# A graph layer on one core: the map to the output moves into the free columns of a PSUM bank that the next range's sums use

## The chip, the cores and the metric

The kernel runs on one core of a Trainium2 chip. Its time is the device time of one execution in microseconds (us). Three timed runs of the kernel before stand at 3958.60, 3969.82 and 3968.54 us, median 3968.54. All durations come from one profiled execution.

## The reference

12,500 nodes of 160 numbers, 400,000 edges sorted by target. Each node row is normalised, cut at zero and mapped; each edge takes its source's mapped row, multiplies it by weights that a small net makes of the edge's 16 features, and by its 4 attributes; the results are summed by target node, mapped to 160 outputs, and added to the node with a skip map:

```
h = maximum(layernorm(x), 0)
y = maps of h;  w = silu(e16 @ W1) @ W2          # per node; per edge
mid = products of w, y[src] and the 4 attributes  # per edge
z = zeros.at[dst].add(mid) / sqrt(10)             # per target node
out = x + C_S * (skip map of h) + C_X * (z @ W_l2)
```

## The kernel before, in words

A first stage (about 107 us) normalises and maps all nodes and writes the mapped rows to a table in memory, `y_d`. All that follows is one loop over 782 batches of four edge tiles (128 edges each, 3125 tiles). The order of every engine's instructions is that in which the code is written; engines wait for each other by semaphores alone.

What a batch b issues, in order: `weigh(b+2)` (edge weights on TensorE into a `pw` buffer, L606, and their scaling on ScalarE, L524); `products(b+1)` (VectorE: L620, L622, L529, L533; they need the gathered rows); the acts left `waiting` by an earlier batch; every 24 batches tables of offsets (`lowest`, `relate`, L199 to L238; the last time `any_far` with L242 and L243, too); `sums(b)`; the gathers (L571); `extras(b)`.

*Gathers.* POOL fetches the 128 source rows of a tile by one indirect transfer, `yg<-y_d,src_q`. A batch's first and third tile have a dependency written by hand (`gather`): the first waits for the last sums of the batch four earlier, the third for the second tile's sums of the batch three earlier. So rows keep step with the sums.

*Sums.* Edges are sorted, so a few tiles in a row touch few nodes. Such a range of 24, 12, 8, 6, 4 or 3 tiles (`wts_of`, from wide to narrow along the edges; 3 in the last 53 of 150 groups) is summed by one matmul per tile (L636) into columns 0 to 319 of a PSUM bank, `pz`. Two such banks alternate. When a range is through, VectorE turns the sums out of the bank with two transposes (L642, L643) into `za`, which holds the four ranges of a group.

*Groups.* A group is four ranges; with ranges of three tiles it is three batches. Before, in the first batch of the next group (k = 0), `linear` maps the group to 160 output columns: five matmuls (L649) into a `px` buffer, a copy to `os` on ScalarE (L651) and a placing matrix `place` on VectorE (L653). At k = 1 `add` places the rows by two matmuls (L661) into another `px` buffer, and `accumulate`, one batch later, adds them to the node's row in `acc` (L672, two instructions). `px` has two buffers, which the hidden layer (L585), the skip map and the look-ups also use. Early stores of finished nodes begin after batch `first_of[GE] + K - 1`.

Of the kernel before, what the change touches and what calls it, by code (L numbers as in the profile page):

```python
# [10 lines left out]
F32 = mybir.dt.float32  # L11
# [7 lines left out]
P = 128  # L19
M0 = 64  # L20
M1 = 32
D = M0 + 3 * M1
# [3 lines left out]
PC = 320  # L26
ZC = 448
ZK = 5
GT = 4
BT = 32  # L30
WN = 32
# [3 lines left out]
BLK = 96  # L35
# [16 lines left out]
def kernel(  # L52
# [34 lines left out]
    NG = len(glist)  # L87
    gstart.append(NG)
    NB = (T + GT - 1) // GT
# [29 lines left out]
    GE = NG - LATE  # L119
# [187 lines left out]
    def node_dma(g, n, dma):  # L307

        f = min(g + n, N // P) - g
        if f:  # L310
            dma(slice(g * P, (g + f) * P), slice(0, f), P)
        if f < n:
            dma(slice((g + f) * P, N), slice(f, f + 1), N - (g + f) * P)

    def store(g, n, eng):
        node_dma(g, n, lambda rows, t, p: eng.dma_start(by_tile(out[rows, :]), acc[:p, g + t.start:g + t.stop, :]))

    def by_tile(ap):
        n = ap.shape[0]
        return ap.rearrange("(t p) c -> p t c", p=min(P, n))  # L320
# [215 lines left out]
    with (  # L536
# [9 lines left out]
    ):  # L546
        hids, rows, wts, sels, z_ps, zT, o_sb, prs, sums_ps, summed = ({} for _ in range(10))
        xss, hss, sTs, sps, ohs, ohTs, vals, xTs = ({} for _ in range(8))
        halves = {}
# [12 lines left out]
        def windows_of(g):  # L562
            return -(-glist[g][2] // wts_of[glist[g][0]])
# [62 lines left out]
        def sums(b):  # L626
            pr, sel, g = prs.pop(b), sels.pop(b), group_of[b]
            q, lo, _ = glist[g]
            WT = wts_of[q]
            for k, t in enumerate(tiles_of(b)):  # L630
                w, o = divmod(t - lo, WT)
                if o == 0:
                    z_ps[g, w] = p_z.tile([P, 512], F32, name="pz")
                pz = z_ps[g, w]
                last = o == WT - 1 or t == T - 1
                mm = nc.tensor.matmul(pz[:, 0:PC], sel[:, slot(t), :, :], pr[:, slot(t), :], start=o == 0, stop=last)  # L636
                (halves if k == 1 else summed)[b] = mm.ins.name
                if last:
                    if w == 0:
                        zT[g] = post.tile([P, ZK, P], F32, name="za")  # L640
                    pz, at_w = z_ps.pop((g, w)), slice(WN * w, WN * (w + 1))
                    nc.vector.transpose(zT[g][:, :, at_w], pz[:, D:PC].rearrange("p (k u) -> p k u", k=ZK))  # L642
                    nc.vector.transpose(zT[g][0:32, :, at_w], pz[0:32, 0:D].rearrange("p (k u) -> p k u", k=ZK))  # L643

        def linear(g):
            m, za = WN * windows_of(g), zT.pop(g)
            po = p_x.tile([P, D], F32, name="px")
            for k in range(ZK):
                nc.tensor.matmul(po[:m, :], za[:, k, :m], wo[:, k, :], start=k == 0, stop=k == ZK - 1)  # L649
            os = post.tile([P, D], F32, name="os")  # L650
            nc.scalar.activation(os[:m, :], po[:m, :], AF.Copy)  # L651
            place = post.tile([P, 2, P], F32, name="place")
            nc.vector.tensor_scalar(place.rearrange("p h n -> p (h n)"), iota, at[:, g:g + 1], None, ALU.is_equal)  # L653
            o_sb[g] = os, place

        def add(g):
            m = WN * windows_of(g)
            os, place = o_sb.pop(g)
            ps = p_x.tile([P, 2, D], F32, name="px")
            for h in range(2):  # L660
                nc.tensor.matmul(ps[:, h, :], place[:m, h, :], os[:m, :], start=True, stop=True)  # L661
            sums_ps[g] = ps

        def accumulate(g):
            ps = sums_ps.pop(g)
            least = LOW if g >= GE else 0
            i = nc.values_load(tile_i[0:1, g:g + 1], engines=[mybir.EngineType.DVE], min_val=least, max_val=NT - 2,
                               skip_runtime_bounds_check_because="clamped to these bounds on the chip")
            part = acc[:, least:, :]
            for h in range(2):  # L670
                to = part[:, ds(i + h - least, 1), :]
                nc.vector.scalar_tensor_tensor(to, ps[:, h:h + 1, :], a_sb[:, ds(i + h, 1)], to,  # L672
                                               op0=ALU.mult, op1=ALU.add)
# [108 lines left out]
        SS, MAP = SB * XB + 8, 7  # L782
        xs_of = {x_batch(u) for u in range(XB)}

        K, KB = 3, BLK // GT
        waiting = []

        def left(act):

            if len(waiting) == 2:  # L790
                waiting.pop(0)()
            waiting.append(act)

        def extras(b):

            g = group_of[b]
            k = b - first_of[g]
            q, r = divmod(b, KB)
            u, v = divmod(b, SB)
            su, sv = divmod(b - SS, SK)  # L800
            if b % 2 == 0 and b + 4 < NB:
                s = (b + 4) // 2
                activate(s, hidden(s))
            if g and k == 0:
                linear(g - 1)
            if b == SS - 8:
                skip_load(0)
            skip = skips.get(sv) if 0 <= su < NU else None
            if skip and sv != MAP:
                skip(su)  # L810
            if r == KB - 11 and q + 1 < NQ:
                spread(q + 1, p_x.tile([P, MW], F32, name="px")[:, :windows_in(q + 1)])
            if u < XB:
                if v == 2:
                    hot_turn(u)
                elif v == 7:
                    x_center(u)
                elif v in (9, 10):
                    x_turn(u, HN * (v == 10))
                elif v == 11:  # L820
                    x_map(u, 0)
            if v == 1 and 0 < u <= XB:
                x_map(u - 1, HN)
            if g and k == 1:
                left(lambda: accumulate(g - 1))
                add(g - 1)
            if skip and sv == MAP:
                left(lambda: skip_add(su))
                skip(su)
# [21 lines left out]
        for b in range(NB):  # L851
            g = group_of[b]
            k = b - first_of[g]
            if b + EARLY < NB:
                features(b + EARLY)
            q, r = divmod(b, KB)
            if r == 0:
                e4_load(q + 1)
            if r == KB - 4:
                e4_join(q + 1)  # L860
            u, v = divmod(b, SB)
            su, sv = divmod(b - SS, SK)
# [16 lines left out]
            if early and b > first_of[GE] + K - 1:  # L879
                store(*early.pop(0), nc.sync)  # L880
# [12 lines left out]
        order.close()  # L893


# [2 lines left out]
    with (  # L898
# [5 lines left out]
        with tc.For_i(0, n, 1) as _:  # L904
# [8 lines left out]
            with tc.For_i(0, TP // GT, 1) as g:  # L913
# [32 lines left out]
                for k in range(GT):  # L946
# [4 lines left out]
                    m = fp.tile([P, ZC], F32, name="f_m")  # L951
# [29 lines left out]
            with tc.For_i(0, NT, 1) as i:  # L981
# [13 lines left out]
                po = fpp.tile([P, D], F32, name="f_po")  # L995
# [54 lines left out]
```

## Time and profile before

| what | value |
|---|---|
| median of three timed runs | 3968.54 us |
| profiled execution, its own time | 3957.18 us |
| its span, first to last instruction | 3955.3 us |
| granted TensorE clock, mean | 0.969 |
| first gather of the loop, last gather | 94.7 us, 3936.0 us |

A row of a group reads: line, engine, operation, output<-input, shape, count | busy us, mean ns of one | idle time just before them, and what ended most of it. A row of the waits reads: who <- whom: us in total, times, longest. A row of the timeline: start us, duration us, engine, line, operation, and in brackets the idle time before it and its releaser. A row of a stretch: from:to, its length, busy us of each engine with the count, granted TensorE clock, DMA share, GB/s; asked for one line of the kernel, it has the busy time of that line's engine alone. PE is TensorE, PEld its weight loads, DVE VectorE, ACT ScalarE, POOL GpSimd. A matmul of this kernel counts as two instructions there.

### The profile page before, as it was taken

The page shows a single profiled execution, that of the slowest core. Times are in us where ns is not written, and L with a number is a line of the kernel's source. Part 1 is how long each engine was busy: PE and PEld are TensorE (multiplying, and loading weights), DVE is VectorE, ACT ScalarE, POOL GpSimd, SP SyncE. Part 2 cuts the span into 40 slices and gives each one's busy share as a digit, 9 for nine tenths or more (in the row PEclk, how much of TensorE's full clock was granted, in tenths as well). Part 3 has the DMA queues.
Part 4 walks back from the last instruction along what each step waited for, and adds up shares of the span by engine and source line. Part 5 has one row for each costly group of instructions (what it writes and reads, how often), then busy time and mean ns, then how long its engine had stood idle before and what let it go on. Part 6 is the DMA issues. An engine that isn't in the chain of part 4 may idle for free.

```text
span 3955.3 us, 54096 instructions
## 1 busy us (share of the span) xinstructions
PE 3583.4 (91%) x17202; PEld 2316.8 (59%) x17202; DVE 2747.0 (69%) x6877; ACT 615.2 (16%) x1845; POOL 2963.8 (75%) x3144
## 2 busy tenths in 40 slices
PE   7898899999999888898989989998999989999988
PEld 7555555555566555555555655555655556666655
DVE  7566666666667666666667777777777777777776
ACT  6111111111111111111111111111111111111111
POOL 6777777777777777777777777777777777777766
PEclk9999999999999999999999999999999999999989
DMA  8222222222222322222222232222223222223224
GB/s 233 72 77 78 74 78 76 76 77 73 77 77 76 81 79 78 78 81 79 81 78 79 76 83 78 81 78 74 81 79 83 77 80 77 81 79 83 75 81 124
DMA packets 262503, 329.05 MB, mean 83 GB/s; under 512 B 82888, under 2 KB 212216, under 8 KB 262216
## 3 DMA queue, kind: packets, MB, share of 16 engines
q0 software_dynamic: 150128, 256.23, 24.2%
q1 hardware_dynamic: 111590, 69.02, 6.2%
q8 instruction: 141, 2.31, 0.2%
q14 instruction: 146, 1.20, 0.1%
q10 hardware_dynamic: 498, 0.30, 0.0%
HBM read 307.67 MB, written 17.61 MB: 82 GB/s over the span
## 4 chain that ended last, share of the span: by engine, by line
PE 38%; DMA 23%; DVE 20%; issue 12%; POOL 7%; DVEq 1%; SPq 1%; ACT 0%; POOLq 0%; ACTq 0%
DMA yg<-y_d,src_q 22%; PE pz L636 20%; DVE pr L533 7%; PE pw L606 7%; POOL yg L571 7%; DVE pr L529 5%; PE px L585 4%; PE px L649 3%; DVE acc L672 1%; DVE za L642 1%; DVE za L643 1%; PE px L661 1%; DVE at L215 1%; DMA acc<-in_x 1%; DVEq L672 0%
## 5 line engine op out<-in xcount | busy, mean ns | idle before, releaser
L571 POOL DMA_INDIRECT yg<-y_d,src_q x3061 | 2897.9, 947 | 950.5 <-issue 636.7
L636 PE MATMUL pz<-pr,sel 128*128 128x320 f32 x6250 | 1972.0, 460 | 23.7 <-DVE za L643 23.7
L636 PEld LDWEIGHTS pz<-pr,sel 128*128 128x128 f32 x6250 | 1165.0, 196 | 606.7 <-issue 239.3
L529 DVE TENSOR_TENSOR pr<-pw,yg 128x512 f32<-128x512 f32 x766 | 527.8, 689 | 919.9 <-DMA yg<-y_d,src_q 919.1
L606 PE MATMUL pw<-w,hT 64*128 64x192 f32 x6250 | 733.8, 353 | 253.3 <-DVE pr L533 222.6
L606 PEld LDWEIGHTS pw<-w,hT 64*128 64x128 f32 x6250 | 505.5, 189 | 548.0 <-issue 372.2
L533 DVE TENSOR_TENSOR pr<-pw,yg 128x384 f32<-128x384 f32 x1532 | 774.0, 546 | 0.0
L622 DVE TENSOR_TENSOR sel<-own,pw 128x512 f32<-128x512 f32 x782 | 536.7, 686 | 27.0
L585 PE MATMUL px<-xe,w 32*128 32x512 f32 x782 | 439.1, 642 | 24.8 <-issue 21.4
L590 ACT ACTIVATE hT<-px 128x512 f32<-128x512 f32 x391 | 233.3, 597 | 1308.7 <-PE px L585 1308.7
L524 ACT ACTIVATE pw<-ev 128x20 f32<-128x20 f32 x782 | 149.1, 191 | 1381.6 <-PE pw L606 1219.2
L642 DVE STREAM_TRANSPOSE za<-pz 128x160 f32<-128x160 f32 x598 | 202.5, 339 | 169.4 <-PE pz L636 167.8
L649 PEld LDWEIGHTS px<-wo,za 128*128 128x128 f32 x1500 | 213.8, 192 | 118.7 <-issue 66.6
L649 PE MATMUL px<-wo,za 128*128 128x160 f32 x1500 | 245.1, 311 | 19.0 <-DVE high L182 8.1
L585 PEld LDWEIGHTS px<-xe,w 32*128 32x128 f32 x782 | 114.5, 183 | 200.7 <-issue 187.8
L643 DVE STREAM_TRANSPOSE za<-pz 32x160 f32<-32x160 f32 x598 | 202.1, 338 | 20.5
L620 DVE TENSOR_TENSOR own<-iota,pw 128x128 f32<-128x128 f32 x782 | 198.3, 254 | 13.7 <-ACT pw L524 10.1
L672 DVE SCALAR_TENSOR_TENSOR acc<-px,a_sb,acc 128x160 f32 x300 | 113.6, 379 | 9.5 <-PE px L661 3.9
L661 PE MATMUL px<-os,place 128*128 128x160 f32 x600 | 113.1, 311 | 7.7 <-DVE place L653 4.8
L661 PEld LDWEIGHTS px<-os,place 128*128 128x128 f32 x600 | 91.6, 192 | 42.2 <-issue 25.4
L651 ACT ACTIVATE os<-px 128x160 f32<-128x160 f32 x150 | 45.5, 303 | 253.1 <-PE px L649 253.1
L347 POOL DMA_INDIRECT xr<-in_x,xi x64 | 61.0, 953 | 21.9 <-issue 11.9
(128 smaller groups left out, 1312.7 us busy)
## 6 DMA issues: line engine op xcount, KB each, us to landing
yg<-y_d,src_q POOLq DMA_INDIRECT x3061
xe<-in_e SPq DMA_DIRECT2D x784, 32.0 KB
xs<-in_x SPq DMA_DIRECT2D x48, 160.0 KB
acc<-in_x SPq DMA_DIRECT2D x11, 640.0 KB
y_d<-ys SPq DMA_DIRECT2D x11, 640.0 KB
out<-acc SPq DMA_DIRECT2D x11, 640.0 KB
raw<-in_e SPq DMA_DIRECT2D x32, 192.0 KB
src_q<-in_src SPq DMA_DIRECT2D x32, 48.0 KB
```

What stands on the lines that cost most here:

```text
L529: nc.vector.tensor_mul(pr[:, :n, :].rearrange("p t (x u) -> p t x u", x=2)[:, :, :, 0:M0], wt[:, :n, 0:NW].rearrange("p t (x u) -> p t x u ...
L533: nc.vector.tensor_mul(pr[:, :n, D * x + M0:D * (x + 1)].rearrange("p t (c u) -> p t c u", c=3), wt[:, :n, 96 * x + M0:96 * (x + 1)].unsqu ...
L571: fetch = nc.gpsimd.indirect_dma_start(out=yg[:, slot(t), :], out_offset=None, in_=y_d, in_offset=bass.IndirectOffsetOnAxis(ap=ev4[t // BL ...
L585: nc.tensor.matmul(ph, w1[r, :], xe[r, :], start=True, stop=True)
L590: nc.scalar.activation(hT, ph, AF.Silu, scale=1.0 / math.sqrt(FC_IN))
L606: nc.tensor.matmul(pw[:, k, 0:NW], hT[r, o:o + P], w2[r, :], start=True, stop=True)
L622: nc.vector.tensor_tensor(sel, own[:, :n, :].unsqueeze(2).to_broadcast([P, n, 4, WN]), wt[:, :n, NW:NW + 4].unsqueeze(3).to_broadcast([P, ...
L636: mm = nc.tensor.matmul(pz[:, 0:PC], sel[:, slot(t), :, :], pr[:, slot(t), :], start=o == 0, stop=last)
L642: nc.vector.transpose(zT[g][:, :, at_w], pz[:, D:PC].rearrange("p (k u) -> p k u", k=ZK))
L643: nc.vector.transpose(zT[g][0:32, :, at_w], pz[0:32, 0:D].rearrange("p (k u) -> p k u", k=ZK))
L649: nc.tensor.matmul(po[:m, :], za[:, k, :m], wo[:, k, :], start=k == 0, stop=k == ZK - 1)
L661: nc.tensor.matmul(ps[:, h, :], place[:m, h, :], os[:m, :], start=True, stop=True)
```

## The change

When a group is finished, it is only put on a list (`owed`, at k = 0). The next range that opens a bank takes it: the five matmuls of the map go into columns 320 to 479 of that bank, ahead of the range's own sums. When that range is through, its two transposes run, then ScalarE copies the map out of the same bank, then `place` is made. `add` follows in the batch after (`adds[b + 1]`), `accumulate` one later. What is left behind the loop is done group by group. `K` becomes 5, which moves the early stores two batches back.

```diff
+                    if owed:
+                        carried[g, w] = owed.pop(0)
+                        linear(carried[g, w], z_ps[g, w][:, PC:PC + D])
...
+                    if (g, w) in carried:
+                        h = carried.pop((g, w))
+                        mapped_out(h)
+                        adds[b + 1] = h
...
-        def linear(g):
+        def linear(g, po):
             m, za = WN * windows_of(g), zT.pop(g)
-            po = p_x.tile([P, D], F32, name="px")
             for k in range(ZK):
                 nc.tensor.matmul(po[:m, :], za[:, k, :m], wo[:, k, :], start=k == 0, stop=k == ZK - 1)
+            pos_of[g] = po
+
+        def mapped_out(g):
+            m, po = WN * windows_of(g), pos_of.pop(g)
             os = post.tile([P, D], F32, name="os")
             nc.scalar.activation(os[:m, :], po[:m, :], AF.Copy)
...
-        K, KB = 3, BLK // GT
+        K, KB = 5, BLK // GT
...
             if g and k == 0:
-                linear(g - 1)
+                owed.append(g - 1)
...
-            if g and k == 1:
-                left(lambda: accumulate(g - 1))
-                add(g - 1)
+            if b in adds:
+                h = adds.pop(b)
+                left(lambda: accumulate(h))
+                add(h)
...
-        for h in ([NG - 2] if NG > 1 else []) + [NG - 1]:
-            for k, stage in enumerate((linear, add, accumulate)):
-                if h == NG - 1 or min(k, 1) > NB - 1 - first_of[NG - 1]:
-                    stage(h)
+        for h in range(NG):
+            if h in finished:
+                continue
+            if h in zT:
+                linear(h, p_x.tile([P, D], F32, name="px"))
+            if h in pos_of:
+                mapped_out(h)
+            if h in o_sb:
+                add(h)
+            accumulate(h)
```

Lines of the changed kernel: map L656, sums L640, copy L662, place L664, placing L672, accumulate L684, edge weights L607, hidden layer L586, transposes L646 and L647.

The order on TensorE near batch 760, where the last table is made (L243 is its matmul). Before:

```order
L636 MATMUL pz<-pr,sel 128x320 x4
L649 MATMUL px<-wo,za 128x160 x5
L606 MATMUL pw<-w_94,hT 128x192 x4
L243 MATMUL px<-one,far 1x1
L636 MATMUL pz<-pr,sel 128x320 x4
L585 MATMUL px<-xe,w_93 128x512
L661 MATMUL px<-os,place 128x160 x2
L606 MATMUL pw<-w_94,hT 128x192 x4
L636 MATMUL pz<-pr,sel 128x320 x4
```

and in the change:

```order
L640 MATMUL pz<-pr,sel 128x320 x4
L672 MATMUL px<-os,place 128x160 x2
L607 MATMUL pw<-w_94,hT 128x192 x4
L243 MATMUL px<-one,far 1x1
L640 MATMUL pz<-pr,sel 128x320 x2
L656 MATMUL pz<-wo,za 128x160 x5
L640 MATMUL pz<-pr,sel 128x320 x2
L586 MATMUL px<-xe,w_93 128x512
L607 MATMUL pw<-w_94,hT 128x192 x4
L640 MATMUL pz<-pr,sel 128x320 x4
```

The map moved from ahead of L243 into the middle of batch 760's sums, now in `pz`; the placing moved from behind these sums to ahead of L243.

On VectorE at the same place (L199 begins the table; L533 ends the products of batch 761). Before:

```order
L529 TENSOR_TENSOR pr<-pw,yg 128x8x64
L533 TENSOR_TENSOR pr<-pw,yg 128x4x96 x2
L199 TENSOR_REDUCE first<-negb 128x5
L200 CAST tile_i<-first 128x5
L201 TENSOR_SCALAR tile_i<-tile_i 128x5
```

and in the change:

```order
L533 TENSOR_TENSOR pr<-pw,yg 128x4x96 x2
L679 TENSOR_LOAD tile_i
L684 ISA x2
L684 SCALAR_TENSOR_TENSOR acc<-px,a_sb,acc 128x160
L684 ISA x2
L684 SCALAR_TENSOR_TENSOR acc<-px,a_sb,acc 128x160
L199 TENSOR_REDUCE first<-negb 128x5
L200 CAST tile_i<-first 128x5
```

An accumulate (of the group before) now stands ahead of the table; before the change the nearest one stood behind the next batch's products.

The end of the loop on TensorE (the `x8` are batches 779 and 780, the single sums batch 781). Before:

```order
L606 MATMUL pw<-w_94,hT 128x192
L636 MATMUL pz<-pr,sel 128x320 x8
L649 MATMUL px<-wo,za 128x160 x5
L636 MATMUL pz<-pr,sel 128x320
L661 MATMUL px<-os,place 128x160 x2
L649 MATMUL px<-wo,za 64x160 x5
L661 MATMUL px<-os,place 128x160 x2
```

and in the change:

```order
L607 MATMUL pw<-w_94,hT 128x192
L640 MATMUL pz<-pr,sel 128x320 x8
L672 MATMUL px<-os,place 128x160 x2
L640 MATMUL pz<-pr,sel 128x320
L656 MATMUL px<-wo,za 128x160 x5
L672 MATMUL px<-os,place 128x160 x2
L656 MATMUL px<-wo,za 64x160 x5
L672 MATMUL px<-os,place 128x160 x2
```

The placing of the last group but two came into the tail, and the last group but one is mapped behind the last sums instead of ahead of them; these two maps still use `px`. In all other 148 groups the copy on ScalarE waits for VectorE's transposes too, and the bank's next range waits for the copy.

More of the change, by code (lines that the diff above doesn't have):

```diff
@@ L548 @@
         xss, hss, sTs, sps, ohs, ohTs, vals, xTs = ({} for _ in range(8))
-        halves = {}
+        halves, pos_of, carried, adds = {}, {}, {}, {}
+        owed, finished = [], set()
         group_of = [g for g, (_, _, n) in enumerate(glist) for _ in range(-(-n // GT))]
@@ L665, in accumulate @@
             ps = sums_ps.pop(g)
+            finished.add(g)
             least = LOW if g >= GE else 0
@@ L879 @@
             if early and b > first_of[GE] + K - 1:
+                assert finished >= set(range(GE))
                 store(*early.pop(0), nc.sync)
@@ L888 @@
         assert SS + NU * SK <= first_of[GE] + K and NQ > 1
-        for h in ([NG - 2] if NG > 1 else []) + [NG - 1]:
-            for k, stage in enumerate((linear, add, accumulate)):
-                if h == NG - 1 or min(k, 1) > NB - 1 - first_of[NG - 1]:
-                    stage(h)
+        for h in range(NG):
[8 more added lines that the diff above has]
+            accumulate(h)
+        assert not carried and finished == set(range(NG))
         order.close()
```

## The prediction

> **What bounds the kernel now.** I read the page from its top and then distrusted it. Busy shares and the chain point at TensorE:
>
> ```profile
> span 3955.3 us, 54096 instructions
> PE 3583.4 (91%) x17202; PEld 2316.8 (59%) x17202; DVE 2747.0 (69%) x6877; ACT 615.2 (16%) x1845; POOL 2963.8 (75%) x3144
> PE 38%; DMA 23%; DVE 20%; issue 12%; POOL 7%; DVEq 1%; SPq 1%; ACT 0%; POOLq 0%; ACTq 0%
> ...
> L571 POOL DMA_INDIRECT yg<-y_d,src_q x3061 | 2897.9, 947 | 950.5 <-issue 636.7
> ```
>
> The last row decides. A gather of one edge tile keeps POOL busy for 947 ns, and the idle ahead of all 3061 of them is 950.5 us, 311 ns each. Busy and idle together are 3848.4 us, 97% of the span, all of it in one in-order engine. So the question is whether those 311 ns are waiting, which a change can remove, or a fixed cost of the next issue. The waits tell it (in total, times, longest):
>
> ```profile
> POOL yg L571 <- issue: 636.7, 2090, 0.3
> ...
> PE pw L606 <- DVE pr L533: 222.6, 193, 5.2
> ...
> POOL yg L571 <- PE pz L636: 68.7, 190, 4.8
> ...
> PE pz L636 <- DVE za L643: 23.7, 27, 3.5
> ```
>
> 2090 gathers waited for nothing that the profile shows, and none longer than 0.3 us: that is a fixed gap. The 190 gathers put down to the sums hold 68.7 us, of which 190 x 0.30 = 57 is the same gap; **about 11.7 us is real waiting for TensorE**, in the whole kernel. Gathers counted by stage say the same:
>
> ```profile
> 1000.00:1500.00 500.00, 377.34 (x400) 0.98 0.29 78
> ...
> 3500.00:3900.00 400.00, 296.70 (x314) 0.96 0.34 93
> ```
>
> 400 gathers in 500 us are 1.25 us each, which is 947 + 0.30. From 3500 to 3900 there are 314 where 320 would fit: the real waiting sits there. TensorE in turn waits mostly for products whose rows have not come (the 222.6 us behind L533), so its 91% is work paced by POOL. A further view shows how early TensorE releases a gather:
>
> ```profile
> 3687.08 2.42 PE L636 MATMUL pz<-pr,sel 128*128 128x320 f32 x8
> ```
>
> ```profile
> 3697.74 0.95 POOL L571 DMA_INDIRECT yg<-y_d,src_q  x1 [0.30 <-DMA yg<-y_d,src_q]
> 3698.99 0.95 POOL L571 DMA_INDIRECT yg<-y_d,src_q  x1 [0.30 <-issue]
> ```
>
> The sums that end at 3689.5 allow the gather of 3697.74, four batches on: a reserve of 8.2 us. Whatever costs TensorE less than its reserve, or saves it anything, does not move POOL.
>
> **The change, part by part.** The moved pieces have these rows:
>
> ```profile
> L649 PE MATMUL px<-wo,za 128*128 128x160 f32 x1500 | 245.1, 311 | 19.0 <-DVE high L182 8.1
> L661 PE MATMUL px<-os,place 128*128 128x160 f32 x600 | 113.1, 311 | 7.7 <-DVE place L653 4.8
> L651 ACT ACTIVATE os<-px 128x160 f32<-128x160 f32 x150 | 45.5, 303 | 253.1 <-PE px L649 253.1
> L642 DVE STREAM_TRANSPOSE za<-pz 128x160 f32<-128x160 f32 x598 | 202.5, 339 | 169.4 <-PE pz L636 167.8
> L672 DVE SCALAR_TENSOR_TENSOR acc<-px,a_sb,acc 128x160 f32 x300 | 113.6, 379 | 9.5 <-PE px L661 3.9
> ```
>
> No instruction is added or lost; 148 of 150 maps change their bank and their place. *Map and px buffer.* A map is 245.1 / 150 = 1.63 us on TensorE before and after. It asks for no px buffer any more; the waits for one that a map met are at most the 19.0 us of its row. TensorE gets back at most these 19.0 and the 23.7 of the bank waits; POOL takes none of it, so: nothing. *The map inside the sums.* With ranges of three tiles it stands between the second and the third tile's sums of the group's second batch, not ahead of all four. The second tile releases its gather 1.6 us earlier, the fourth when it did before; both have reserves like the 8.2 above: nothing, outside the stall below. *The bank's release.* The next range but one now waits for ScalarE's copy as well, which waits for VectorE's transposes: 339 + 338 ns of transposes are followed by 303 ns and two hand-overs of some 0.05 us (an estimate from the tail rows below, where the copy starts 0.04 behind the last map), 0.4 us in 148 places. The nearest row for such a wait is this one:
>
> ```profile
> 3677.12 2.39 PE L636 MATMUL pz<-pr,sel 128*128 128x320 f32 x8 [0.42 <-DVE za L643]
> ```
>
> Here 0.42 us of waiting on the bank passed without a gap on POOL. In the same place the accumulate (2 x 379 ns), which stood ahead of those transposes, now comes two batches later, so the wait should even shrink. I take nothing; the ends are 0 and 148 x 0.4 = 59 us of TensorE time, of which POOL would see what exceeds the reserves. Behind ScalarE's waiting copy stand the hidden layer's activation and the next pw scaling; neither is needed until a later batch's products.
>
> What reaches the end is where the reserve is gone already. **The stall at 3840 us**, in batch 760, where the last table of offsets is made:
>
> ```profile
> 3829.54 1.52 PE L649 MATMUL px<-wo,za 128*128 128x160 f32 x10
> ...
> 3840.92 0.19 PE L243 MATMUL px<-one,far 128*1 128x1 f32 x2 [8.94 <-DVE far L242]
> ...
> 3841.04 4.64 PE L636 MATMUL pz<-pr,sel 128*128 128x320 f32 x8
> ...
> 3843.82 0.94 POOL L571 DMA_INDIRECT yg<-y_d,src_q  x1 [3.74 <-PE pz L636]
> ...
> 3845.61 2.07 PE L585 MATMUL px<-xe,w 32*128 32x512 f32 x2
> ...
> 3847.61 1.44 PE L661 MATMUL px<-os,place 128*128 128x160 f32 x4
> ...
> 3850.56 3.87 PE L636 MATMUL pz<-pr,sel 128*128 128x320 f32 x8
> ...
> 3853.33 0.94 POOL L571 DMA_INDIRECT yg<-y_d,src_q  x1 [4.82 <-PE pz L636]
> ```
>
> ```profile
> 3837.00:3853.00 16.00, 12.08 (x29) 6.94 (x30) 8.15 (x31) 0.79 (x2) 6.25 (x7) 0.50 0.28 82
> ```
>
> POOL loses 3.74 + 4.82 - 2 x 0.30 = 8.0 of the 11.7 us here, and all of it at a granted clock of 0.50. Three things change. The accumulate comes ahead of the table on VectorE: 2 x 0.38 = +0.8. The map, at 1.52 us ahead of the stall in a time when TensorE would wait anyway, falls into the sums at half clock: 2 x 1.5 = +3.0. The placing (1.44) moves out, ahead of the stall: -1.4. That makes +2.4; the clock may come back before the later sums are through, so I take **+2.0**. The ends are +0.9 (the map at full rate, 0.8 + 1.5 - 1.4) and +3.8 (the placing that left frees nothing). [...]
>
> **The tail.** The last group but one no longer finds a range to ride on, and is done whole behind the loop:
>
> ```profile
> 3942.75 1.52 PE L649 MATMUL px<-wo,za 128*128 128x160 f32 x10
> ...
> 3944.11 0.70 PE L636 MATMUL pz<-pr,sel 128*128 128x320 f32 x2
> 3944.31 0.30 ACT L651 ACTIVATE os<-px 128x160 f32<-128x160 f32 x1 [9.02 <-PE px L649]
> 3944.66 0.81 PE L661 MATMUL px<-os,place 128*128 128x160 f32 x4
> ...
> 3945.62 1.57 PE L649 MATMUL px<-wo,za 128*64 128x160 f32 x10
> ...
> 3947.64 0.81 PE L661 MATMUL px<-os,place 64*128 64x160 f32 x4 [0.45 <-ACT os L651]
> 3948.49 0.80 DVE L672 SCALAR_TENSOR_TENSOR acc<-px,a_sb,acc 128x160 f32 x2 [1.53 <-PE px L661]
> ```
>
> Now TensorE has from 3942.75: placing 0.81, last sums 0.70, map 1.52, copy with its hand-overs 0.39 (3944.27 to 3944.66), placing 0.81, last map 1.57: 3948.55. From the end of the last map to the accumulate are 1.30 us (3947.19 to 3948.49), so 3949.85 against 3948.49, +1.4; less some overlap where rows run into each other (1.52 from 3942.75 passes 3944.11 by 0.16): **+1.2**, ends 0.7 and 2.
>
> **Small gaps.** The other 11.7 - 8.0 = 3.7 us of waiting lie in a few places; the largest single one is late:
>
> ```profile
> POOL yg L571 <- PE pz L636: 2.8, 6, 1.3
> ```
>
> This is the stretch 3230 to 3300, one wait of 1.3. A map that stood ahead of those sums now stands behind their second tile; I take that 1.0 back and give 0.2 for early places that placing now falls into: **-0.8**, ends -3.7 and +3.7.
>
> Sum: 2.0 + 1.2 - 0.8 = +2.4 us, 0.06%. The profiled execution took 3957.18 (span 3955.3 and 1.9 around it), so 3959.6. The three timed runs are 3958.60, 3969.82 and 3968.54; the profiled one lies at their low edge. On their median of 3968.54 the forecast is **3971 us**. Scatter of 11 us is 0.28%: a measurement of this kernel tells about 0.3% from no change.
>
> **The rivals.**
> *TensorE is the bound after all (faster).* For it: 91% busy and the chain's 38%. Then the 19.0 and 23.7 us of px and bank waits would come off: 3968.5 - 43 = 3926. Against it: 400 gathers per 500 us with a gap that never exceeds 0.3. Even with every real wait gone POOL gives 11.7 us: 3957. Chance 0.06.
> *The bank's release becomes the bound (slower).* Place: the narrow windows from 3100 us on, 53 groups of three batches, 15 us each.
>
> ```profile
> 3500.00:3900.00 400.00, 372.63 (x1782) 243.62 (x1781) 301.79 (x777) 52.45 (x164) 296.70 (x314) 0.96 0.34 93
> ```
>
> TensorE has (400 - 372.6) / 26.7 groups = 1.0 us of slack per group. Should the chain of transposes, copy and next range cost 1.5 us per group, since the copy queues behind other waiting work on ScalarE, 0.5 x 53 = 27 us come out: 3995, +0.7%. It decides from 1.0 us per group on; my price is 0.4. [...] Chance 0.12.
> *No change that reaches POOL (forecast, +2.4).* Chance 0.82, with all signs within 0.3%.
>
> Range: the low end takes the fast timed run, 3958.6, with the small gaps gone, 3955; the high end takes the slow one, 3970, with the stall at +3.8, the tail at 2, the small gaps at +3.7 and a third of the slower rival's 27 (9): 3988. Faster by over 0.3%: 0.06; within: 0.82; slower: 0.12.
>
> **What would show it.** Right: gathers still at 400 per 500 us, gaps of 0.3; last gather issued 1 to 3 us later than 3936.0, the time between it and the end 1 us longer; map rows gone from the px waits, without a gain. Wrong: POOL waits for the sums well above 68.7 us from 3100 on (slower rival), or a gather period below 1.25 us (then the fixed gap was none).

## The result, and the profile after

The kernel before: 3965.63 us, median of 17 runs (3958.60 to 3970.71). The changed kernel: 3974.62 us, median of 17 (3971.64 to 3977.49). The ratio is 1.0020, 95% interval [1.0013, 1.0027]: slower by 5 to 11 us, within the 0.3% that the forecast called no change, on the side to which its sum pointed (+2.4 us), and almost four times as far.

The page of the changed kernel, in the order in which that of before was read: the span, the busy shares, the chain that ended last, and the group of the gathers.

```profile
span 3972.8 us, 54151 instructions
PE 3554.2 (89%) x17202; PEld 2304.5 (58%) x17202; DVE 2742.9 (69%) x6877; ACT 601.9 (15%) x1845; POOL 2972.8 (75%) x3144
PE 30%; DMA 26%; DVE 21%; issue 13%; POOL 9%; DVEq 1%; ACT 0%; SPq 0%; POOLq 0%; ACTq 0%
...
L572 POOL DMA_INDIRECT yg<-y_d,src_q x3061 | 2906.9, 950 | 954.8 <-issue 659.5
```

Busy and idle of the gathers are 3861.7 us, 97% of the span, as before. The waits of POOL (who <- whom: us in total, times, longest), first of the whole kernel, then of 100 to 1350 us alone, changed kernel and kernel before:

```profile
POOL yg L572 <- issue: 659.5, 2163, 0.3
POOL yg L572 <- PE pz L640: 54.2, 143, 4.3
POOL yg L572 <- DVE za L647: 41.8, 135, 1.0
```

```profile
POOL yg L572 <- PE pz L640: 21.2, 53, 2.1
...
POOL yg L572 <- DVE pr L533: 8.1, 17, 3.2
```

```profile
POOL yg L571 <- PE pz L636: 16.2, 47, 1.2
```

The fixed gap is 0.305 us (659.5 / 2163), so what exceeds it is real waiting: 54.2 - 143 x 0.305 = 10.6 behind the sums, 41.8 - 135 x 0.305 = 0.6 behind the transposes. Taken over all 3061 gathers, the idle beyond 0.305 us in gaps above 0.4 us (the start left out) is 14.2 us, against 12.1 before. The sum hides two moves in opposite directions: in the early stretch (21.2 - 53 x 0.305) + (8.1 - 17 x 0.305) = 7.9 us, against 3.1 before (1.9 behind the sums in the row above, the rest in two single waits on VectorE); in the stall of the last table 6.3, against 8.0.

The profiled executions lie further apart than the medians, 3974.62 against 3957.18: that of before is below every one of its 17 timed runs. Their spans differ by 17.5 us, which the trace splits like this:

| piece | before | after | difference |
|---|---|---|---|
| first gather of the loop | 94.68 | 97.06 | +2.4 |
| 3061 gathers, mean busy ns of one | 946.7 | 949.65 | +8.9 |
| real waiting between gathers, us | 12.1 | 14.2 | +2.1 |
| last gather to the end, us | 19.35 | 22.68 | +3.3 |

The rest, 0.8, lies in the fixed gaps, 0.2 ns more in each. Two pieces sit where the change does something, +2.1 and +3.3. The largest, 3 ns on each gather, is the one that had to be put to the test.

**The early stretch.** A table of offsets in the wide ranges, near 1320 us. First TensorE, VectorE and POOL of the kernel before (rows left out):

```profile
1316.34 1.12 PE L585 MATMUL px<-xe,w 32*128 32x512 f32 x2
...
1317.39 1.62 PE L649 MATMUL px<-wo,za 128*128 128x160 f32 x10
...
1317.92 0.15 DVE L199 TENSOR_REDUCE first<-negb 128x3 f32<-128x12 f32 x1
...
1325.12 0.92 PE L606 MATMUL pw<-w,hT 64*128 64x192 f32 x8 [1.47 <-DVE pr L533]
...
1325.97 2.42 PE L636 MATMUL pz<-pr,sel 128*128 128x320 f32 x8
...
1327.59 0.94 POOL L571 DMA_INDIRECT yg<-y_d,src_q  x1 [0.41 <-PE pz L636]
```

and the same place in the changed kernel:

```profile
1325.82 0.15 DVE L199 TENSOR_REDUCE first<-negb 128x3 f32<-128x12 f32 x1
...
1332.78 0.92 PE L607 MATMUL pw<-w,hT 64*128 64x192 f32 x8 [2.59 <-DVE pr L533]
...
1333.63 2.85 PE L656 MATMUL pz<-wo,za 128*128 128x160 f32 x10
...
1336.27 2.81 PE L640 MATMUL pz<-pr,sel 128*128 128x320 f32 x8
...
1338.28 0.95 POOL L572 DMA_INDIRECT yg<-y_d,src_q  x1 [3.19 <-DVE pr L533]
```

Before, the map ran ahead of the delay that VectorE's table makes, in time that TensorE would have waited away; the next sums came at once. In the change the map has to wait until a range opens its bank, behind the table: TensorE waits 2.59 instead of 1.47 for the delayed products, behind that wait the granted clock is 0.55 (1333.6 to 1336.3; the map takes 2.85 and not 1.62), and only then come the sums that release the gather. POOL waits 3.19 - 0.30 = 2.9 us where it waited 0.1.

What this place costs was not the same in two executions of the changed kernel, and the map did not take as long in both. In the second (the control of the third set) TensorE waits 2.56 here, the map takes 1.63, as in the kernel before (1.62), and POOL waits 1.2 us:

```profile
1333.45 1.63 PE L656 MATMUL pz<-wo,za 128*128 128x160 f32 x10
...
1336.42 0.94 POOL L572 DMA_INDIRECT yg<-y_d,src_q  x1 [1.51 <-PE pz L640]
```

With the maps of the wide ranges put back (third set), the place is as before the change:

```profile
1331.23 0.92 PE L607 MATMUL pw<-w,hT 64*128 64x192 f32 x8 [1.49 <-DVE pr L533]
...
1333.70 0.94 POOL L572 DMA_INDIRECT yg<-y_d,src_q  x1 [0.41 <-PE pz L640]
```

At other early places it is not the map. Near 886 us of the changed kernel a placing stands ahead of the sums that POOL waits for; before the change no placing stood there and POOL did not wait:

```profile
883.51 0.81 PE L672 MATMUL px<-os,place 128*128 128x160 f32 x4
...
886.72 0.95 POOL L572 DMA_INDIRECT yg<-y_d,src_q  x1 [1.04 <-PE pz L640]
```

A placing stands ahead of the sums at 658 us, too, where POOL waits 2.09 instead of 1.11. Against the kernel before, the two placings cost some 1.7 us of POOL's waiting and the maps at two places (near 1109 and 1338 us) some 3.9; the other early places give some 0.9 back.

**The stall of the last table,** POOL and TensorE of the changed kernel:

```profile
3857.14 0.19 PE L243 MATMUL px<-one,far 128*1 128x1 f32 x2 [9.48 <-DVE far L242]
3857.26 2.50 PE L640 MATMUL pz<-pr,sel 128*128 128x320 f32 x4
3859.56 2.87 PE L656 MATMUL pz<-wo,za 128*128 128x160 f32 x10
3862.22 1.69 PE L640 MATMUL pz<-pr,sel 128*128 128x320 f32 x4
```

```profile
3860.03 0.95 POOL L572 DMA_INDIRECT yg<-y_d,src_q  x1 [4.26 <-PE pz L640]
...
3864.19 0.95 POOL L572 DMA_INDIRECT yg<-y_d,src_q  x1 [1.95 <-PE pz L640]
...
3867.36 1.01 POOL L572 DMA_INDIRECT yg<-y_d,src_q  x1 [0.97 <-DVE za L647]
```

The map is there at half clock as forecast (2.87 at a granted clock of 0.50, 3859.56 to 3862.43), and the first wait is 0.5 longer (4.26 against 3.74). But the second is 1.95, not 4.82: the granted clock is full again from 3863.1 on.

```profile
3862.00:3863.00 1.00, 1.00 (x4) 0.80 (x4) 0.94 (x3) 0.00 (x0) 0.24 (x1) 0.50 0.17 43
3863.00:3864.00 1.00, 1.00 (x4) 0.44 (x4) 0.00 (x0) 0.00 (x0) 0.00 (x0) 0.94 0.20 51
```

That is 6.0 us after TensorE resumed at 3857.14. In the kernel before it took 12.6, from 3840.92 to 3853.5:

```profile
3852.00:3853.00 1.00, 1.00 (x3) 0.61 (x3) 0.69 (x2) 0.00 (x0) 0.00 (x0) 0.50 1.04 317
3853.00:3854.00 1.00, 1.00 (x5) 0.64 (x3) 0.00 (x0) 0.00 (x0) 0.67 (x1) 0.74 1.02 272
```

TensorE was busy throughout in both (5.96 of 5.96 us from 3857.14, 12.58 of 12.58 from 3840.92).

**The tail** of the changed kernel:

```profile
3950.15 0.95 POOL L572 DMA_INDIRECT yg<-y_d,src_q  x1 [0.30 <-issue]
...
3953.89 0.30 ACT L662 ACTIVATE os<-pz 128x160 f32<-128x160 f32 x1 [4.85 <-DVE za L647]
...
3954.25 3.65 PE L640 MATMUL pz<-pr,sel 128*128 128x320 f32 x8 [2.79 <-ACT os L662]
...
3957.69 1.21 PE L672 MATMUL px<-os,place 128*128 128x160 f32 x4
...
3963.95 0.81 PE L672 MATMUL px<-os,place 64*128 64x160 f32 x4 [0.45 <-ACT os L662]
3964.80 0.80 DVE L684 SCALAR_TENSOR_TENSOR acc<-px,a_sb,acc 128x160 f32 x2 [1.69 <-PE px L672]
3966.14 0.38 SPq L316 DMA_DIRECT2D out<-acc  x1
3967.37 3.20 ACTq L316 DMA_DIRECT2D out<-acc  x2
```

The sums of batch 780 in the kernel before:

```profile
3940.52 2.39 PE L636 MATMUL pz<-pr,sel 128*128 128x320 f32 x8 [3.16 <-DVE za L643]
```

From the last gather to the last placing are 13.80 us, against 11.67 before (3935.97 to 3947.64): +2.1, of which some 1.7 are a lower clock (sums of batch 780: 3.65 at a granted clock of 0.64, against 2.39 at 1.00; a placing: 1.21 at 0.58, against 0.81 at 1.00). Of the rest the order behind these sums makes +0.9, and -0.45 comes from the sums, which begin that much sooner after the last gather. From that placing to the end are 8.9 us against 7.7, +1.2; here the final store on ScalarE's queue is issued 2.57 us after the last accumulate began, against 1.36.

### The profile page after: what moved, and what is told of

It is laid out like the page before. It is cut to its first block, busy times and chain, and to the rows that moved or that the text cites. A ratio compares the mean times of both kernels' runs of the same rounds, so it can differ in the third digit from the quotient of the medians.

```text
span 3972.8 us, 54151 instructions
## 1 busy us (share of the span) xinstructions
PE 3554.2 (89%) x17202; PEld 2304.5 (58%) x17202; DVE 2742.9 (69%) x6877; ACT 601.9 (15%) x1845; POOL 2972.8 (75%) x3144
## 4 chain that ended last, share of the span: by engine, by line
PE 30%; DMA 26%; DVE 21%; issue 13%; POOL 9%; DVEq 1%; ACT 0%; SPq 0%; POOLq 0%; ACTq 0%
DMA yg<-y_d,src_q 25%; PE pz L640 16%; POOL yg L572 9%; DVE pr L533 8%; PE pw L607 6%; DVE pr L529 6%; PE px L586 3%; PE pz L656 2%; DVE acc L684 1%; DVE za L647 1%; DVE za L646 1%; PE px L672 1%; DVE at L215 1%; DVEq L684 1%; DVEq L529 0%
## 5 line engine op out<-in xcount | busy, mean ns | idle before, releaser
L572 POOL DMA_INDIRECT yg<-y_d,src_q x3061 | 2906.9, 950 | 954.8 <-issue 659.5
L640 PE MATMUL pz<-pr,sel 128*128 128x320 f32 x6250 | 1956.8, 455 | 19.8 <-DVE za L647 15.5
L640 PEld LDWEIGHTS pz<-pr,sel 128*128 128x128 f32 x6250 | 1154.2, 195 | 566.9 <-issue 207.3
L607 PE MATMUL pw<-w,hT 64*128 64x192 f32 x6250 | 730.5, 351 | 329.8 <-DVE pr L533 286.6
L607 PEld LDWEIGHTS pw<-w,hT 64*128 64x128 f32 x6250 | 506.3, 188 | 662.0 <-issue 489.0
L533 DVE TENSOR_TENSOR pr<-pw,yg 128x384 f32<-128x384 f32 x1532 | 774.1, 547 | 0.0
L586 PE MATMUL px<-xe,w 32*128 32x512 f32 x782 | 437.0, 640 | 8.5 <-issue 7.4
L646 DVE STREAM_TRANSPOSE za<-pz 128x160 f32<-128x160 f32 x598 | 203.9, 341 | 152.0 <-PE pz L640 150.2
L656 PE MATMUL pz<-wo,za 128*128 128x160 f32 x1480 | 240.6, 311 | 0.0
L656 PEld LDWEIGHTS pz<-wo,za 128*128 128x128 f32 x1480 | 217.1, 195 | 29.6 <-issue 19.2
L586 PEld LDWEIGHTS px<-xe,w 32*128 32x128 f32 x782 | 114.2, 183 | 182.6 <-issue 173.9
L647 DVE STREAM_TRANSPOSE za<-pz 32x160 f32<-32x160 f32 x598 | 202.0, 338 | 20.5
L672 PEld LDWEIGHTS px<-os,place 128*128 128x128 f32 x600 | 89.4, 191 | 101.6 <-issue 63.0
L662 ACT ACTIVATE os<-pz 128x160 f32<-128x160 f32 x148 | 45.0, 304 | 597.1 <-DVE za L647 548.8
L672 PE MATMUL px<-os,place 128*128 128x160 f32 x600 | 117.9, 319 | 16.4 <-DVE acc L727 8.0
L684 DVE SCALAR_TENSOR_TENSOR acc<-px,a_sb,acc 128x160 f32 x300 | 113.7, 379 | 11.8 <-PE px L672 6.4
```

The costliest lines, as they stand in the source:

```text
L533: nc.vector.tensor_mul(pr[:, :n, D * x + M0:D * (x + 1)].rearrange("p t (c u) -> p t c u", c=3), wt[:, :n, 96 * x + M0:96 * (x + 1)].unsqu ...
L572: fetch = nc.gpsimd.indirect_dma_start(out=yg[:, slot(t), :], out_offset=None, in_=y_d, in_offset=bass.IndirectOffsetOnAxis(ap=ev4[t // BL ...
L586: nc.tensor.matmul(ph, w1[r, :], xe[r, :], start=True, stop=True)
L607: nc.tensor.matmul(pw[:, k, 0:NW], hT[r, o:o + P], w2[r, :], start=True, stop=True)
```

## The experiments

Three theories. The first (1, or A): the map lost the cover of VectorE's tables in the wide ranges, and the tail got longer; POOL pays both. The second (2, or B): something in the changed program makes each gather some 3 ns longer. The third is the prediction's slower rival: the bank's later release. In the expectations of the first set theory 1 says, beside that, that the longer gathers belong to the execution and not to the program. The first two sets of kernels ran on two chips on which every kernel of this study takes about 4660 us, the kernel before too (4661.44 and 4666.44 us); the third set ran on one where the kernel before takes 3963.48. Each kernel left one profile. Ratios are always to runs of the kernel before on the same chip.

### First set: the two kernels again, and a longer lead of the gathers

Both kernels unaltered:

> The kernel before, unchanged, as a second profiled execution. Theory 1 (the gap between the two profiles of 17.4 us is mostly the execution, not the change): the mean gather on POOL differs from the first profile's 947 ns, by up to 3 ns, and the ratio is within 0.1% of 1. Theory 2 (the change itself lengthens every gather by 3 ns): the gather stays at 946 to 947 ns here. POOL's real waiting for the sums stays near 12 us in both.

> The changed kernel as a second profiled execution. Theory 1: the mean gather lies in the same band as that of the kernel before on this chip, within 1 ns; real waits of POOL near 14 us. Theory 2: 949 to 950 ns, 3 ns over the kernel before on the same chip. Both: ratio 1.001 to 1.003.

Measured: 4662.73 us, ratio 0.9997 [0.9987, 1.0007] for the kernel before against itself; 4661.07 us, 0.9997 [0.9988, 1.0007] for the change. On this chip the change costs nothing, where 1.001 to 1.003 was expected. The same page of the kernel before shows what is different there:

```profile
span 4659.5 us, 54096 instructions
PE 3885.9 (83%) x17202; PEld 2489.2 (53%) x17202; DVE 2738.2 (59%) x6877; ACT 588.3 (13%) x1845; POOL 2965.9 (64%) x3144
PE 69%; another core or an unknown queue 11%; DVE 8%; issue 8%; ACT 2%; DVEq 0%; DMA 0%; ACTq 0%; POOL 0%
L571 POOL DMA_INDIRECT yg<-y_d,src_q x3061 | 2900.0, 947 | 1630.9 <-issue 763.9
```

A gather takes 947 ns as ever, but POOL's idle is 1630.9 instead of 950.5 us, so it waits some 680 us more, not the 12 that were expected. The chain now runs through TensorE (69%) and through a releaser that the profile cannot name (11%), and the granted clock is 0.90 on average, not 0.969. By the chain TensorE is the bound here, not POOL, though it is busy for only 83% of the span; the profile does not say why it stands still in the rest. So this chip cannot show what POOL's gaps of 10 us are worth. It does settle theory 2: the mean gather is 947.4 ns in the kernel before and 947.2 in the change. The 3 ns do not come with the program.

Gathers six batches ahead of the sums instead of four, in both kernels:

```diff
-AHEAD = 4
+AHEAD = 6
...
-    ygp = ctx.enter_context(tc.tile_pool(name="yg", bufs=6))
+    ygp = ctx.enter_context(tc.tile_pool(name="yg", bufs=8))
```

> The kernel before with gathers six batches ahead of the sums in place of four (eight row buffers in place of six). Theory 1 (POOL's issue is the bound and loses time only where the reserve runs out): the waits of some 12 us go, except perhaps 2 at the stall of the last table; time 9 to 12 us under the kernel before, ratio 0.997 to 0.998. Rival (TensorE is the bound): no change, ratio within 0.1% of 1.

> The changed kernel with gathers six batches ahead. Theory 1: the waits of some 14 us go, and what stays between this and the kernel before with the same lead is the tail alone, 1 to 4 us (0.03 to 0.1%). Theory 2: 9 us more stay, 0.25 to 0.35% between the two. Rival (the bank's release holds TensorE up in the narrow ranges): waits of POOL from 3100 us on remain.

Measured: 4679.13 us, 1.0039 [1.0025, 1.0053] on the kernel before; 4667.69 us, 1.0011 [1.0003, 1.0020] on the change. The expected gain did not come. That fits TensorE as the bound, where a longer lead would have nothing to give; why it costs 0.4% on the kernel before was not followed up. The question had to be asked again on another chip (third set).

### Second set: one part of the change at a time

Groups with wide ranges mapped as before the change, in `px` and in the next group's first batch; only narrow ranges carry a map in their bank:

```diff
             if g and k == 0:
-                owed.append(g - 1)
+                if wts_of[glist[g - 1][0]] >= 6:
+                    linear(g - 1, p_x.tile([P, D], F32, name="px"))
+                    mapped_out(g - 1)
+                    adds[b + 1] = g - 1
+                else:
+                    owed.append(g - 1)
```

> The changed kernel, but groups with ranges of 6 tiles or more (45 of 150) are mapped into a px buffer in the next group's first batch, as before the change; only narrow ranges carry a map. Theory 1 (the loss sits where a map or a placing that used to fill the wait for VectorE's table now falls behind it, in the wide ranges, and in the tail): POOL's real waits up to 1400 us go back from 7.9 to 3 to 5 us, time 3 to 5 us under the changed kernel, ratio to before near 1.001. Rival (the bank's release in narrow ranges): no change against the changed kernel, 1.002. On a chip where TensorE is the bound, as in the first four runs, all ratios within 0.1% of 1.

Measured: 4655.76 us, 0.9979 [0.9969, 0.9989].

The same, and the last group but one mapped in the loop:

```diff
-                if wts_of[glist[g - 1][0]] >= 6:
+                if wts_of[glist[g - 1][0]] >= 6 or g == NG - 1:
```

> As the one before, and the last group but one is also mapped in its next group's first batch, so that the tail is that of the kernel before. Theory 1: 1 to 3 us less again, time from the last gather to the end 19 to 20 us in place of 22.7, ratio to before 1.000 to 1.0005. Rival: 1.002.

Measured: 4657.81 us, 0.9979 [0.9969, 0.9988].

The map at the change's place in the order, but in a `px` buffer and copied out at once, so that the bank of the sums is left alone:

```diff
-                        linear(carried[g, w], z_ps[g, w][:, PC:PC + D])
+                        linear(carried[g, w], p_x.tile([P, D], F32, name="px"))
+                        mapped_out(carried[g, w])
...
-                        h = carried.pop((g, w))
-                        mapped_out(h)
-                        adds[b + 1] = h
+                        adds[b + 1] = carried.pop((g, w))
```

> The changed kernel, but the map goes into a px buffer at the place in TensorE's order where the change makes it, and is copied out at once: the delay without the shared bank. Theory 1 (the later place costs, not the bank): as the changed kernel, ratio 1.001 to 1.003, the same waits of POOL in the first 1400 us. Rival (the bank's release): as the kernel before, 1.000.

Measured: 4664.79 us, 0.9995 [0.9985, 1.0006].

The change with the bank held longer, by two more copies out of it on ScalarE in each of 148 places (0.6 us a place, an estimate from the 304 ns of a copy in the change; from 100 to 4700 us ScalarE is busy for 593.5 us, against 533.5 in the change of the first set, which is 0.4 a place):

```diff
+            for _ in range(2):
+                spare = post.tile([P, D], F32, name="spare")
+                nc.scalar.activation(spare[:m, :], po[:m, :], AF.Copy)
```

> The changed kernel with two further copies of the map by ScalarE, ahead of the real one, so that the bank stays taken 0.6 us longer in 148 places. Theory 1: hidden in TensorE's reserve, except two times 0.6 in the tail: 1 to 2 us over the changed kernel, ratio 1.002 to 1.003. Rival (the bank's release is on the path in the 53 groups of narrow ranges): 0.6 x 53 = 32 us over it, ratio 1.010.

Measured: 4672.21 us, 1.0011 [1.0001, 1.0021].

What follows, all of it on a chip of the pace of the first set's (mean granted clock 0.90 in all four kernels), and on which the change itself was not run: the bank as such is worth nothing that can be told, since the map at the same place in a buffer of its own gives 0.9995, as the change gives 0.9997 in the first set. (A cost of 0.1 to 0.3% was expected of both. Neither shows one, so this pair cannot tell the later place from the bank.) Holding the bank longer, by 60 us going by ScalarE's busy time or 148 x 0.6 = 89 by the estimate, costs 0.14% more than the change in the first set, about 6.5 us (the two intervals overlap). The waits of the sums on the copy are 31.5 us with it and 30.2 in the change there, so the longer hold itself is hidden. The place of the maps in the wide ranges does count: with them put back the kernel takes 4655.76 us, against 4664.79 with all maps at the later place in `px`, 0.2%, where at most 0.1% was expected of such a chip. It is also 0.2% faster than the kernel before, so there what is left of the change, the narrow ranges for the most part, gains something; this was not followed up. All this points to the first theory, though where POOL is not the bound it says nothing of POOL.

### Third set: the same questions where POOL is the bound

> The changed kernel unaltered, as a control for the three runs beside it. Theory A (the map now falls behind VectorE's table in the wide ranges, and the last groups stand later behind the loop): on a chip where the kernel before takes about 3965 us POOL's own waiting shows and the ratio is 1.001 to 1.003; on a chip where it takes about 4660 us TensorE is the bound and the ratio is 0.999 to 1.001. Theory B (the gather itself lasts some 3 ns longer in the changed program): a mean gather of 949 ns or more beside 947 in the kernel before, on either chip.

Measured: 3972.43 us, 1.0024 [1.0015, 1.0033]. The result is met again, +9 us.

> Groups whose ranges have six tiles or more are mapped into px in the first batch of the next group as before the change; only the narrow ranges carry a map in the bank. Theory A: at about 3965 us per run the early gaps come back to those of the kernel before (some 4.8 us less than in the change), the later tail stays, so the ratio is about 1.0005 (0.9995 to 1.0015), below the control of the same set by 0.0008 to 0.0015; at about 4660 us 0.998, as the first run of this kernel there. Theory B: no difference from the control at about 3965 us.

Measured: 3966.15 us, 1.0007 [0.9998, 1.0016].

> As the kernel beside it, and the last group but one is mapped in the loop as before, too. Theory A: at about 3965 us per run also the tail's 3 us come back: ratio 0.9997 (0.9985 to 1.0005), the time from the last gather to the end about 19 to 20 us instead of 22.7; at about 4660 us 0.998. Theory B: no difference from the control.

Measured: 3965.51 us, 1.0006 [0.9997, 1.0015].

The last of these with the longer lead of the first set:

> The kernel beside it with gathers allowed six batches ahead of the sums instead of four (eight yg buffers instead of six). If POOL's gather issue is the bound (a chip with about 3965 us per run), only its real waiting of some 10 us can go: ratio 0.997 (0.996 to 0.9985), the waits of gathers on sums that exceed 0.4 us nearly gone. If TensorE is the bound there as well, no gain from it: 0.9995 or more. At about 4660 us per run: 0.998 to 1.001.

Measured: 3955.46 us (3954.12 to 3957.08), 0.9978 [0.9969, 0.9987].

The waits of gathers on sums in these four, one row of each kernel in the order above:

```profile
POOL yg L572 <- PE pz L640: 68.1, 184, 4.3
```

```profile
POOL yg L572 <- PE pz L640: 55.0, 155, 4.3
```

```profile
POOL yg L572 <- PE pz L640: 59.2, 174, 4.3
```

```profile
POOL yg L572 <- PE pz L640: 61.0, 200, 0.3
```

Less the fixed gap these are 12.0, 7.7, 6.1 and 0.0 us. In the last one 200 x 0.305 is the whole row: POOL never waits for TensorE. Of all 3061 gathers:

| kernel | median us | real waiting us | mean gather ns | last gather to the end us |
|---|---|---|---|---|
| change | 3972.43 | 15.7 | 947.3 | 22.7 |
| wide ranges back | 3966.15 | 8.9 | 948.7 | 21.1 |
| and last group but one back | 3965.51 | 6.9 | 949.1 | 21.1 |
| and lead 6 | 3955.46 | 0.0 | 949.4 | 19.65 |

The first theory holds where it spoke of the wide ranges: with their maps and placings back 6.8 us of POOL's waiting and 6.3 us of the time are gone. Not all of that is theirs. In the early stretch the waiting falls from 8.5 to 3.8 us, 4.7. In the control another 1.4 are a single wait at 3260 us, in the narrow ranges, where the edit changes nothing: the sums there took 3.43 us for four tiles, and in the other kernel 2.42. The last 0.6 lie in the stall. The tail is 1.6 shorter, for the most part because the final store is not late there, and the edit does not explain that. The second half of the theory does not hold: the last group but one at its old place gains nothing that can be told (0.6 us), and the tail stays at 21.1. What the tail pays for shows beside the kernel with lead 6, which has the same order of instructions there. The sums of batch 780 in the one and in the other:

```profile
3946.70 4.11 PE L640 MATMUL pz<-pr,sel 128*128 128x320 f32 x8 [2.70 <-ACT os L662]
```

```profile
3939.68 2.42 PE L640 MATMUL pz<-pr,sel 128*128 128x320 f32 x8 [2.83 <-ACT os L662]
```

The wait ahead is about as long in both; the granted clock around these sums is 0.68 in the first (3945 to 3950) and 1.00 in the second (3938 to 3943). The sums differ by 1.7 us, and the tails by 1.5. Theory 2 falls here as well: the control has 947.3 ns and the slow result, the three faster kernels have longer gathers. The mean gather moves by 3 ns from execution to execution, 9 us in all, without following any edit.

The lead of six does on this chip what the first set could not show: 10 us, just the waiting that was left (6.9) and the shorter tail (1.5), with a start that came 1.2 earlier. It beats both the change and the kernel before: 3955.46 against 3963.48.

## Why the prediction was right, and where it was off

*The bound* was read rightly. POOL's fixed pace is 3060 x (949.4 + 304.8) ns = 3838 us; with 97.5 ahead of it and 19.65 behind, that is the 3955 us of the kernel whose gathers never wait. What the orders of TensorE's work tried here gave or took is the 7 to 16 us of waiting above and some 3 us of the tail. On the chip of the first set the faster rival's premise (TensorE is the bound) is true by the chain, and even there the change as a whole gave nothing (0.9997).

*Map and px buffer: nothing.* Right. The map's row now has no idle time ahead of it, and POOL gained nothing from that:

```profile
L656 PE MATMUL pz<-wo,za 128*128 128x160 f32 x1480 | 240.6, 311 | 0.0
```

*The bank's release: nothing, ends 0 and 59 us of TensorE.* Right. In the changed kernel all waits of sums on the copy come to 3.7 us:

```profile
L640 PE MATMUL pz<-pr,sel 128*128 128x320 f32 x6250 | 1956.8, 455 | 19.8 <-DVE za L647 15.5 <-ACT os L662 3.7
```

19.8 us of bank waits in all, against 23.7 before. Of the 3.7, 2.79 stand in the tail, where nothing hides them: the sums of batch 780 start 0.45 us behind the end of the transposes, against 0.15 in the kernel before. So the copy costs 0.3 us there, near the price of 0.4. Holding the bank 0.4 to 0.6 us longer cost 0.1% on the chip of the second set. The slower rival falls.

*Small gaps: -0.8.* This is the step that failed: the measured term is (14.2 - 6.3) - (12.1 - 8.0) = +3.8, just beyond its upper end of +3.7. The late 1.0 us at 3254 was given back in this profile, but in the control POOL loses 1.4 us at the same place, behind sums of 3.43 us, so that gain was at least in part luck of the execution. And "0.2 for early places that placing now falls into" stands against 4.8 us: placing did it at two places, with some 1.7, and at two others the map, with some 3.9, for which the term had nothing. The prediction took its reserve of 8.2 us from a place with ranges of three tiles and let it stand for all. In the wide ranges a table of offsets on VectorE eats that reserve more than once, and there map and placing had been work that filled TensorE's wait, or had stood elsewhere. The prediction saw that cover for the last table (1.52 us "in a time when TensorE would wait anyway") and did not look for it at the earlier ones. The kernel with the wide maps put back shows it: 4.7 us of early waiting are gone. It moves the placings back as well, so it does not part the two.

*The stall: +2.0.* Mis-sized, with the wrong sign: -1.7 (6.3 against 8.0), in the control -2.3. The parts are as argued: the accumulate ahead of the table (the wait for it 9.48 against 8.94 us), the map at half clock (2.87 at 0.50), the placing gone from there. What failed is the clock behind them, taken to stay at half for as long as before. The clock was back 6.0 us after TensorE resumed, and in the control at about 3856.9, 4.8 us after its 3852.05:

```profile
3850.00:3856.00 6.00, 3.95 (x12) 3.13 (x13) 3.16 (x17) 0.00 (x0) 1.62 (x2) 0.50 0.14 34
3856.00:3862.00 6.00, 6.00 (x27) 3.90 (x26) 2.78 (x7) 1.08 (x3) 3.17 (x4) 0.93 0.21 55
```

No run here shows what decides between these 4.8 and 6.0 us and the 12.6 of before. In the 12.6 us matmuls of 32 and 64 rows (L585 at 3845.61, 2.07 us; L606 at 3848.97, 1.65 us) stand in the middle, in the other two only matmuls of 128 rows; that this is the cause is not shown.

*The tail: +1.2.* Mis-sized: +3.3. The order behind the sums gave 0.9, near its price, by the trace, and the sooner start of the sums took 0.45 of it back; the clock of 0.64 and 0.58 in these sums and the next placing 1.7; the later final store 1.2. The last two were not in the sum. That the maps' order is not the cost was shown (21.1 us with either order); what delays ScalarE's store by 1.2 us in the change and its control, and not in the three other kernels of the third set, stays open, and so does what sets the clock.

*Sum.* Stall -1.7, tail +3.3 and small gaps +3.8 are +5.4 us, against +2.4 forecast; in the control -2.3, +3.4 and (15.7 - 5.7) - 4.1 = +5.9 are +7.0. The medians differ by 9.0 in both. The remaining 2 to 4 us were not traced to an edit. That the forecast time came so near, 3971 against 3974.62, is partly luck: its base, 3968.54, lay 2.9 above the median of 17 runs, and the errors of the terms (-3.7 in the stall, +2.1 in the tail, +4.6 in the small gaps) partly cancel. The first gather of all five later profiles at this pace starts at 97.1 to 98.8 us, against 94.7 in the only such profile of the kernel before; on the slow chip the kernel before starts later than the change (116.8 against 115.4). One profile does not tell whether that is the change.

*The signs.* From 1000 to 1500 us the changed kernel issued 396 gathers, not 400; two of the long early waits lie there. The last gather came 14.2 us later than 3936.0, not 1 to 3, of which 8.9 are the longer gathers of that execution and 2.4 its later start. The waits on sums from 3100 us on, the sign of the slower rival, did not grow: 19.6 us against 27.5 before.

## What to carry to other kernels

A reserve read at one place holds for that place. Before work is moved away from where it stands, look in every stage at what it was standing in for: here five matmuls of 1.6 us, and placings of 0.8, were free only because they ran where another engine was late or where there was reserve. Where one engine's fixed pace is the bound and its waits are few, a longer lead for that engine (10 us here) was worth more than any order of the others' work that was tried.

## What the runs showed of the hardware

The same program took 3966 us in the runs of the result, 3963 on the chip of the third set, and 4661 and 4666 on two others, with gathers of 947 to 950 ns in the profiles of the result and of the first and third set. On the first of those two the chain of the kernel before lies 69% on TensorE instead of 38%, with a busy share of 83% instead of 91%; the mean granted clock is 0.90 on both (0.896 to 0.906 in eight kernels) instead of 0.97. What holds TensorE up the profile does not name, and it stays open. The wide maps put back are worth 0.2% against the change on the chip of the third set, and 0.2% on a slower one against all maps at the later place. But a lead of six batches gained 0.25% on the one kind of chip and cost 0.1 to 0.4% on the other.

The time from TensorE's return to work until its clock was full again behind the last table of offsets was 4.8, 6.0 and 12.6 us in three executions, with TensorE busy all that time. After waits of 2.7 to 3.2 us in the tail the sums of batch 780 took 3.65 us in the change (granted clock 0.64) and 4.11 in the kernel with both places put back (0.68 from 3945 to 3950), and 2.42 with lead 6 and 2.39 in the kernel before (1.00 in both), the last behind the longest of these waits.
